# A third buffer for a unit's evacuated products, against shorter rings of sums, in a deformable-convolution block

## The chip, the cores and the metric

The kernel runs on one core of one Trainium2 chip. The metric is the device time of one execution in microseconds, the median of several runs. The profile is of one execution, whose span on the chip is 7707.8 us. PE is the matrix engine (TensorE), DVE is VectorE, ACT is ScalarE, POOL is GpSimd, and SP is the queue that issues nearly all DMAs.

## The reference

The input `x` is (2, 256, 128, 128) in fp32. The first layer normalises `x` by groups of channels, and runs three branches with dilations 1, 9 and 12. A branch computes 18 offsets per pixel by a 3x3 convolution, samples the image bilinearly at the nine displaced positions, and sums the nine samples with one weight per channel and tap. Then follow a norm over channels and a GELU. The three branches and a 1x1 convolution are added and go through a norm, a two-layer MLP and another norm. The second layer is a group norm and a 3x3 convolution with ternary weights. Cut to what matters here:

```
def _deform_dw(x, offset, w, pad, dil):
    ...
    py = yy[None, None] - pad + ky[None, :, None, None] * dil + off[:, :, 0]
    px = xx[None, None] - pad + kx[None, :, None, None] * dil + off[:, :, 1]
    sampled = _bilinear(x, py, px)
    wk = w.reshape(C, K)
    return jnp.einsum('bckhw,ck->bchw', sampled, wk)
def _branch(x, w_off, w_def, lw, lb, pad, dil):
    off = _conv(x, w_off, pad, dil)
    y = _deform_dw(x, off, w_def, pad, dil)
    return jax.nn.gelu(_ln2d(y, lw, lb), approximate=False)
...
out = _ln2d(x1 + x2 + x3 + c, n1_w, n1_b)
h = gelu(h @ mlp_w1.T + mlp_b1) @ mlp_w2.T + mlp_b2
```

## The kernel before

The kernel has three stages. The first writes a padded, transposed image to a table in DRAM, computes the offsets, and stores them as hat functions of the distance to each sampling position (`hats`), one set for y and one for x. The second samples and does the rest of the first layer. The third is the second layer's convolution. The change is in the second stage, `sample_near`, which takes the larger part of the time.

Sampling is done as a matrix product. A *unit* is an image, a pair of rows `Rt` and a branch `br`: 2 x 67 x 3 = 402 units. For a unit, DVE multiplies the hats in y with those in x into a matrix `A` (`build`, L813), once for each of the three kernel rows `ky`; the hats come by two loads, `hy` and `hx` (L793), with three buffers each, so that one unit fills them. The image's patches `xs` (L767) come as 14 loads for each pair of rows, into 20 buffers. A unit has two *samples*, one for each half of the channels (`sample(u, c)`). In a sample, PE multiplies the 14 patches by `A` (L886) in pairs, each pair into a PSUM bank `pm` (four banks); ACT copies each bank into `ev` (L895), the unit's evacuated products, in seven copies; and DVE adds them, tap by tap with a weight per channel, to sums held in a ring (`accumulate`, L864). The first product that reaches a row of the ring is written by ACT (L857) in place of an addition.

There is one ring for each branch, of `RINGS[br]` image rows (L50). A row `y` lies at `y % n_ring`. Two neighbouring rows are added by one instruction unless they cross the end of the ring, where the instruction is cut in two. When four rows (a *group*) have all their sums, the group's *tail* begins: PE transposes it out of the ring, ACT copies the transposes, and norms, GELU and, after the third branch, the MLP follow. The tails are advanced a step at a time between the samples by `tail.advance()`, so that their instructions are mixed with those of the sampling. If a new row would fall on ring rows whose group has not yet been transposed, the code advances the tail until it has:

```
while owner and owner != (b, br, m // R) and owner not in tail.read:
    tail.advance()
```

Nearly all instructions of PE, DVE and ACT in this stage are pinned to the order of the program (`pin`). On DVE the order within a unit is: the sums of the first half, then the builds of the unit after next (`prepare(u + 2)`), then the sums of the second half. `A` has two buffers, used in turn by the units. `ev` has two buffers:

```
ev = pool.tile([P, 9 * RI, NT * CI], F32, name="ev", tag="ev", bufs=2)
```

so ACT's first copy of a sample waits until DVE has done with the sums of the sample before the last. `load_hats(u + 1)` follows `prepare(u)`, and a scheduler sets the order of the loads on SP.

Of the kernel before, what the change touches and what calls it, by code (L numbers as in the profile page):

```python
# [9 lines left out]
F32 = mybir.dt.float32  # L10
# [9 lines left out]
P = 128  # L20
# [21 lines left out]
RI, CI = 2, 10  # L42
TR, TC = RI + 2 * REACH, CI + 2 * REACH
NT = -(-(W + 2 * REACH) // CI)
# [2 lines left out]
WA = 28 + W  # L47
NH = TR + TC
HALF = 64
RINGS = (12, 28, 32)  # L50
BRS = (0, 1, 2)
NORMS = 3
VBUFS = 9
# [14 lines left out]
def conv_preact_kernel(ctx: ExitStack, tc: tile.TileContext, t: dict, out: bass.AP):  # L68
# [680 lines left out]
    def sample_near(pool, psum, k):  # L749
# [26 lines left out]
        def taps(u):  # L776
            return [ky for ky in (-1, 0, 1) if valid(units[u][1], units[u][2], ky)]
# [43 lines left out]
        def accumulate(u, c, ev, kys):  # L821
# [4 lines left out]
            ring = k["rings"][br]  # L826
            n_ring = RINGS[br]
            sums = {ky: [] for ky in kys}
# [37 lines left out]
        def sample(u, c):  # L866

            b, Rt, br = units[u]
            kys = taps(u)
            tail.advance()  # L870
            if not kys:
                tail.advance()
                if c == KC - 1:
                    prepare(u + 2)
                return
            A = k["A"][u % len(k["A"])].rearrange("p t i w -> p (t i) w")
            m0, m1 = (kys[0] + 1) * 3 * RI, (kys[-1] + 2) * 3 * RI
            n = (m1 - m0) * CI
            ev = pool.tile([P, 9 * RI, NT * CI], F32, name="ev", tag="ev", bufs=2)
            for T in range(0, NT, 2):  # L880
                if T // 2 == NT // 4:
                    tail.advance()
                pm = psum.tile([P, 2, 256], F32, name="pm", tag="pm", bufs=4)
                for j in range(2):
                    pin(
                        nc.tensor.matmul(  # L886
                            pm[:, j, 0:n],
                            lhsT=xts[b, Rt][T + j][:, c * P : (c + 1) * P],
                            rhs=A[:, m0:m1, AO + (T + j) * CI : AO + (T + j + 1) * CI],
                            start=True,  # L890
                            stop=True,
                        )
                    )
                pin(
                    nc.scalar.copy(  # L895
                        ev[:, m0:m1, T * CI : (T + 2) * CI].rearrange(
                            "p m (t j) -> p t m j", j=CI
                        ),
                        pm[:, :, 0:n].rearrange("p t (m j) -> p t m j", j=CI),
                    )  # L900
                )
            if c == KC - 1:
                prepare(u + 2)
            accumulate(u, c, ev, kys)

        def prepare(u):

            if u < len(units):
                for ky in taps(u):
                    build(u, ky)  # L910
                if u + 1 < len(units):
                    load_hats(u + 1)
# [5 lines left out]
        for u, (b, Rt, br) in enumerate(units):  # L918
            if br == BRS[0] and u + len(BRS) < len(units):
                load_tiles(*units[u + len(BRS)][0:2])  # L920
            for c in range(KC):
                sample(u, c)

            while done[b, br] < NGRP and (
                Rt == NR - 1
                or (done[b, br] + 1) * R - 1 < (Rt + 1) * RI - REACH - DILS[br]
            ):
                g = done[b, br]
                r0 = g * R % RINGS[br]
                ring = k["rings"][br][:, :, r0 : r0 + R, :].rearrange("p k r w -> p k (r w)")  # L930
                tail.begin(tail.branch(b, br, g, ring), LAG)
                done[b, br] += 1
# [93 lines left out]
    with tc.If(beyond > 0) as cmp:  # L1026
        with ExitStack() as bctx:
            psum = bctx.enter_context(tc.tile_pool(name="ps_g", bufs=1, space=PSUM))
            pool = bctx.enter_context(tc.tile_pool(name="gpool", bufs=1))
            for b in range(NB):  # L1030
                sample_any(b, pool, psum)
    with cmp.Else():
        with ExitStack() as bctx:
            psum = bctx.enter_context(tc.tile_pool(name="ps_b", bufs=1, space=PSUM))
            pool = bctx.enter_context(tc.tile_pool(name="bpool", bufs=1))
# [3 lines left out]
            k["rings"] = [  # L1039
                pool.tile([P, KC, n, W], F32, name=f"ring{i}") for i, n in enumerate(RINGS)  # L1040
            ]
# [273 lines left out]
```

## Time and profile before

| | |
|---|---|
| median of 3 runs | 7720.23 us (7712.4 to 7721.3) |
| span of the profiled execution | 7707.8 us |
| PE busy | 7056.2 us, 92% |
| DVE busy | 6136.7 us, 80% |
| ACT busy | 4821.4 us, 63% |
| DMA, mean over the span | 215 GB/s |

Busy times are unions over the whole span, so they mix three stages with different limits. In the group lines of the page, the part after the first bar is the busy time in us and the mean duration of one instruction in ns (these overlap on PE), and the part after the second bar is the engine's idle time just before these instructions and what ended most of it. A line of the waits gives the waiting engine and its line, what it waited for, the total in us, how often, and the longest. A line of the timeline gives start and duration in us, and in square brackets the engine's idle time before it. A line of the windows gives for each stretch the busy time of PE, PE's weight load, DVE, ACT and POOL with their instructions, and then the granted clock of PE, the busy share of the DMA engines and GB/s.

### The profile page before, as it was taken

The numbers are of one execution on the slowest core, as the hardware profiler recorded it, in microseconds if no ns is written. First come the engines' busy times: TensorE is split into PE (matmuls) and PEld (weight loads), VectorE is DVE, ScalarE is ACT, GpSimd is POOL, SyncE is SP. The second block draws the span as 40 slices with busy tenths as digits, with TensorE's granted clock in tenths as the row PEclk, the third lists the DMA queues.
The fourth block names the chain that finished last, engine by engine and source line by source line (L and its number), as shares of the span: only waits on it lengthen the run. The fifth ranks groups of instructions, "written<-read, shape, count | busy, mean of one in ns | idle before, by whom it ended". The sixth has DMA issues, their size and how long they took to land. (4 is left out here: it accounts for less than half of the span.)

```text
span 7707.8 us, 115349 instructions
## 1 busy us (share of the span) xinstructions
PE 7056.2 (92%) x37984; PEld 5364.4 (70%) x37984; DVE 6136.7 (80%) x12907; ACT 4821.4 (63%) x10150; POOL 716.3 (9%) x1292
## 2 busy tenths in 40 slices
PE   6899888999999999999988999999999999899999
PEld 3455477877877787877777877877788877444444
DVE  7666658888888888888578888888888886677676
ACT  2344356777777777777666777777777777433232
POOL 0000000111111111111100111111111111000000
PEclk9899989999999999999999999999999999899999
DMA  9867699999999999998689999999999996222121
GB/s 296 242 188 200 181 233 252 243 254 257 248 250 254 255 246 249 248 255 228 190 232 249 250 250 258 248 251 252 251 249 251 246 250 172 86 77 73 71 74 49
DMA packets 1012350, 1658.94 MB, mean 215 GB/s; under 512 B 120672, under 2 KB 573072, under 8 KB 1007512
## 3 DMA queue, kind: packets, MB, share of 16 engines
q1 hardware_dynamic: 994328, 1617.86, 78.2%
q10 hardware_dynamic: 17408, 33.56, 1.3%
q8 instruction: 304, 4.98, 0.3%
q14 instruction: 310, 2.54, 0.1%
HBM read 1381.02 MB, written 270.06 MB: 214 GB/s over the span
## 5 line engine op out<-in xcount | busy, mean ns | idle before, releaser
L886 PE MATMUL pm<-A,xs 128*128 128x180 f32 (+2 forms) x22288 | 3603.7, 317 | 467.9 <-ACT ev L895 435.2
L886 PEld LDWEIGHTS pm<-A,xs 128*128 128x128 f32 x22288 | 3399.3, 195 | 684.4 <-ACT ev L895 543.7
L864 DVE SCALAR_TENSOR_TENSOR ring<-ev,defw,ring 128x256 f32<-128x256 f32 (+3 forms) x6272 | 2775.7, 462 | 358.6 <-ACT ev L895 173.4
L895 ACT COPY ev<-pm 128x360 f32<-128x360 f32 (+2 forms) x5572 | 2238.5, 455 | 1125.7 <-DVE ring L864 453.7
L813 DVE TENSOR_TENSOR A<-hy,hx 128x768 f32<-128x768 f32 x1130 | 1021.3, 946 | 417.4 <-DMA hx<-hats 238.6
L1169 PE MATMUL pc<-cring,signs 128*128 128x512 bf16 x4608 | 1007.5, 382 | 20.0 <-ACT cring L1116 13.3
L1169 PEld LDWEIGHTS <-signs 128*128 128x128 bf16 x4608 | 452.4, 98 | 574.5 <-issue 30.1
L611 ACT ACTIVATE T<-T,rs 128x256 f32<-128x256 f32 x1280 | 662.4, 593 | 3.3 <-POOL rs L607 3.2
L604 POOL TENSOR_SCALAR rs<-mv 128x4 f32<-128x4 f32 x320 | 122.5, 383 | 4962.3 <-DVE mv L602 2297.5
L570 PE MATMUL hp<-T,w 128*128 128x512 f32 x1024 | 493.1, 606 | 13.8 <-ACT T L689 13.8
L600 DVE BATCH_NORM_STATS2 st<-T 128x6 f32<-128x256 f32 x1280 | 447.0, 412 | 24.0 <-ACT T L592 23.9
L320 PE MATMUL pz<-wz,xa 128*128 128x486 f32 x1024 | 462.8, 585 | 1.3 <-DVE zr L327 1.3
L570 PE MATMUL h<-hT,w 128*128 128x512 f32 x1024 | 460.1, 592 | 0.0
L639 ACT ACTIVATE T<-zc,bb,bw 128x512 f32<-128x512 f32 x384 | 279.2, 782 | 219.8 <-PE zc L623 215.4
L857 ACT ACTIVATE ring<-ev,defw 128x256 f32<-128x256 f32 (+1 forms) x788 | 392.2, 503 | 24.1
L623 PEld LDWEIGHTS zc<-ident,T 128*128 128x128 f32 x2560 | 323.4, 150 | 97.2 <-issue 61.4
L1177 ACT ACTIVATE o<-xl,l1b 128x1024 f32<-128x1024 f32 x64 | 73.5, 1148 | 502.0 <-DMA out_x<-o 384.6
L623 PE MATMUL zc<-ident,T 128*128 128x128 f32 x2560 | 365.9, 287 | 20.2 <-ACT T L611 14.1
L606 POOL TENSOR_TENSOR rs<-rs,mhalf 128x4 f32<-128x4 f32 x320 | 371.3, 1160 | 0.0
L1116 ACT CAST cring<-D 128x2048 bf16<-128x2048 f32 (+1 forms) x140 | 245.0, 1755 | 185.0 <-PE pc L1169 127.6
L592 ACT COPY T<-tp 128x512 f32<-128x512 f32 x640 | 341.9, 590 | 29.5 <-PE tp L590 29.2
L427 ACT ACTIVATE hb<-ph 96x512 f32<-96x512 f32 (+1 forms) x384 | 211.2, 592 | 183.0 <-PE ph L419 177.0
(118 smaller groups left out, 5258.8 us busy)
## 6 DMA issues: line engine op xcount, KB each, us to landing
hy<-hats SPq DMA_DIRECT2D x1114, 384.0 KB
hx<-hats SPq DMA_DIRECT2D x1114, 384.0 KB
xs<-table SPq DMA_DIRECT2D x1876, 128.0 KB
g12d<-T SPq DMA_DIRECT2D x128, 512.0 KB
other<-g12d SPq DMA_DIRECT2D x128, 512.0 KB
hats<-hb SPq DMA_DIRECT2D x192, 240.0 KB
hats<-hb SPq DMA_DIRECT2D x192, 192.0 KB
xl<-x1d SPq DMA_DIRECT2D x56, 640.0 KB
```

The costliest lines, as they stand in the source:

```text
L320: nc.tensor.matmul(pz[:, 0:NZ], lhsT=xt[:, c, r, :], rhs=k["wz"][:, c, :], start=c == 0, stop=c == KC - 1,)
L570: nc.tensor.matmul(out, lhsT=w, rhs=v, start=i == 0, stop=i == n - 1)
L600: pin(nc.vector.bn_stats(st[:, j, :], Tv[:, j, :]))
L606: nc.gpsimd.tensor_tensor(rs[:, 0, :], rs[:, 0, :], mhalf[:, 0:NB4], ALU.pow)
L611: nc.scalar.activation(Tv[:, j, :], Tv[:, j, :], AF.Identity, scale=rs[:, 0, j : j + 1], bias=rs[:, 1, j : j + 1],)
L623: nc.tensor.transpose(zc[:, j * P : (j + 1) * P], Tv[:, j, c * P : (c + 1) * P], ident)
L813: nc.vector.tensor_tensor(dst, hy[:, i0:i1].rearrange("p i t w -> p t i w"), hx[:, i0:i1].rearrange("p i t w -> p t i w"), ALU.mult,)
L857: pin(nc.scalar.mul(dst, src, w))
L864: pin(nc.vector.scalar_tensor_tensor(dst, src, w, dst, ALU.mult, ALU.add))
L886: nc.tensor.matmul(pm[:, j, 0:n], lhsT=xts[b, Rt][T + j][:, c * P : (c + 1) * P], rhs=A[:, m0:m1, AO + (T + j) * CI : AO + (T + j + 1) * C ...
L895: nc.scalar.copy(ev[:, m0:m1, T * CI : (T + 2) * CI].rearrange("p m (t j) -> p t m j", j=CI), pm[:, :, 0:n].rearrange("p t (m j) -> p t m ...
L1169: nc.tensor.matmul(pc[:, bank, :], lhsT=w[:, m * P : (m + 1) * P], rhs=xc[:, i, k, t * JC : (t + 1) * JC, kx : kx + W], start=j == 0, stop ...
```

## The change

`ev` gets a third buffer, and two rings lose four rows each. Each `ev` buffer takes 18 x 140 x 4 = 10080 bytes of a partition, and a ring row 2 x 128 x 4 = 1024 bytes, so eight rows are 8192 bytes.

```diff
-RINGS = (12, 28, 32)
+RINGS = (8, 24, 32)
...
-            ev = pool.tile([P, 9 * RI, NT * CI], F32, name="ev", tag="ev", bufs=2)
+            ev = pool.tile([P, 9 * RI, NT * CI], F32, name="ev", tag="ev", bufs=3)
```

ACT's first copy of a sample then waits for the sums of the sample three before it. In the rings of dilation 1 and dilation 9 a group's rows are taken again one group earlier, and row pairs cross the end of these rings more often.

## The prediction

> **What bounds the kernel now.** I read the page's slices first, to find the stage that the change touches.
>
> ```profile
> PE   6899888999999999999988999999999999899999
> DVE  7666658888888888888578888888888886677676
> DMA  9867699999999999998689999999999996222121
> GB/s 296 242 188 200 181 233 252 243 254 257 248 250 254 255 246 249 248 255 228 190 232 249 250 250 258 248 251 252 251 249 251 246 250 172 86 77 73 71 74 49
> ```
>
> A slice is 193 us. Slices 6 to 33 are the sampling stage, with PE at 9, DVE at 8 and DMA at 9 at once; no engine stands alone. The dip in the middle is where image 0 ends and image 1 begins. Then the groups:
>
> ```profile
> L886 PE MATMUL pm<-A,xs 128*128 128x180 f32 (+2 forms) x22288 | 3603.7, 317 | 467.9 <-ACT ev L895 435.2
> L864 DVE SCALAR_TENSOR_TENSOR ring<-ev,defw,ring 128x256 f32<-128x256 f32 (+3 forms) x6272 | 2775.7, 462 | 358.6 <-ACT ev L895 173.4
> L895 ACT COPY ev<-pm 128x360 f32<-128x360 f32 (+2 forms) x5572 | 2238.5, 455 | 1125.7 <-DVE ring L864 453.7
> ```
>
> The chain of releases is the point: PE waits for ACT to empty a PSUM bank (435.2 us), and ACT waits for DVE to finish with an `ev` (453.7 us). The waits in the even part of the stage, 2000 to 3500 us:
>
> ```profile
> ACT ev L895 <- PE pm L886: 113.3, 51, 3.0
> PE pm L886 <- ACT ev L895: 100.7, 67, 3.1
> ACT ev L895 <- DVE ring L864: 99.1, 65, 2.9
> DVE ring L864 <- ACT ev L895: 42.4, 25, 2.1
> DVE A L813 <- DMA hx<-hats: 36.6, 33, 2.9
> DVE A L813 <- PE pm L886: 35.8, 14, 2.6
> ```
>
> PE idles 104 us of these 1500 (busy 1395.9), and 100.7 of it is this one wait. DVE waits for PE and ACT (42.4 + 35.8 + 18.5 for h = 96.7 us), and for hats (36.6). So each waits for the other, at different places. The timeline shows where. The work repeats: the same 2.56 us wait stands at 3045.33 and 3131.77, so a period (two row steps, six units) is 86.4 us.
>
> ```profile
> 3131.77 2.70 DVE L813 TENSOR_TENSOR A<-hy,hx 128x768 f32<-128x768 f32 x3 [2.56 <-PE pm L886]
> 2107.41 3.77 DVE L864 SCALAR_TENSOR_TENSOR ring<-ev,defw,ring 128x256 f32<-128x256 f32 x8 [2.08 <-ACT ev L895]
> 2134.21 1.19 ACT L895 COPY ev<-pm 128x360 f32<-128x360 f32 x3 [2.16 <-DVE ring L864]
> 2134.72 2.10 PE L886 MATMUL pm<-A,xs 128*128 128x180 f32 x12 [2.38 <-ACT ev L895]
> 2146.11 3.12 ACT L895 COPY ev<-pm 128x360 f32<-128x360 f32 x7 [2.01 <-DVE ring L864]
> 2146.63 2.10 PE L886 MATMUL pm<-A,xs 128*128 128x180 f32 x12 [1.12 <-ACT ev L895]
> 2154.12 1.19 ACT L895 COPY ev<-pm 128x360 f32<-128x360 f32 x3 [1.43 <-DVE ring L864]
> 2154.64 2.10 PE L886 MATMUL pm<-A,xs 128*128 128x180 f32 x12 [2.59 <-ACT ev L895]
> ```
>
> From 2107 to 2154 DVE runs without a wait for PE or ACT and holds both back; in the other 39 us of the period PE works on the tail's long matmuls, and DVE waits. Two buffers let ACT be one sample ahead, which is too little to carry PE over the DVE-heavy part. One whole period by windows:
>
> ```profile
> 2107.00:2193.40 86.40, 79.63 (x461) 67.83 (x460) 75.59 (x171) 65.13 (x145) 11.37 (x20) 1.00 0.96 251
> ```
>
> **What the Trainium skill says.** "Perfetto Trace Analysis", Optimization Strategy: the same gap coming back on the engine that should be saturated can mean too few buffers. That is this picture: three PE gaps in each period, each just after ACT's wait for an `ev`. The same page, Identifying the Most-Contended Engine, calls DMA occupancy misleading, since there are 16 engines. The trace agrees: in stretches of 5 us the share goes up to 1.12, so I use bytes. "VectorE: DVE Perf Modes", The TRN2 errata, says that an operation on SBUF pays a fixed cost per instruction. Here 128x256 takes 481 ns and 128x128 takes 346 ns, so halving a row pair costs 2 x 346 - 481 = 211 ns.
>
> **The change part by part.**
>
> *Third `ev`.* ACT's first copy of sample s then waits for the sums of sample s-3, not s-2. One sum of 8 instructions (3.8 us) and what DVE does beside it lie between the two. The waits to be removed are 2.2 us at most, so all of them go at the present timing. What PE gets back is the smaller of each pair above: 2.16 + 1.12 + 1.43 = 4.7 us per period. The rest of PE's gaps (0.2, 1.2 and 0.4 us at 2106.35) is ACT busy with copies of the tail, and stays. PE's floor is 86.4 - 4.7 = 81.7 us.
>
> *The other floors.* DVE's waits for PE and ACT in this period are 4.1 + 2.6 + 0.7 = 7.4 us (waits by engine), so DVE could do it in 79.0, plus 0.3 for the splits below. DMA moves 251 GB/s x 86.4 us = 21.7 MB; over the 188 of 290 five-us windows with a share of 1.00 or more the rate was 267 GB/s on average, so it needs 81.2 us even if never idle. Three floors within 2.5 us mean that none will be met. Hats are the weak point: `hy` and `hx` have three buffers each, which one unit fills, so the next unit's loads cannot start before this unit's builds. I take two thirds of the 4.7: 3.1 us per period, a period of 83.3 us at 260 GB/s. The share is a choice: at nothing, DMA bounds; at all of it, PE does.
>
> *How many periods.* Even stretches are 1450 to 3450 and 4200 to 6200 us: 4000 / 86.4 = 46.3. So 46.3 x 3.1 = 144 us. At the starts of the images (1200 to 1450, 3950 to 4200) DVE is held by hats (27.0 and 37.9 us of 250) and by neither PE nor ACT (under 4 us); the waits for `ev` there are slack, so I count nothing. Ends of images: nothing, up to 10 us.
>
> *Shorter rings: splits.* A row pair that crosses a ring's end is cut in two. Counted from the built program: 64 of 128x256 become 128 of 128x128, and 8 of 2x122 become 16 of 122: 64 x 0.211 + 8 x (2 x 0.338 - 0.473) = 15.1 us of DVE. In the even stretches DVE has 7.4 us of slack per period against 0.3. On the path: some 2 us, at the starts. Bounds: 0 and 15.
>
> *Shorter rings: waits.* The rows of a ring are taken again a group earlier, and the code then advances the tail until the old rows have been transposed. In the built programs PE, ACT and POOL have the same instructions in the same order before and after, so no advance is forced. ACT writes the first product of a new row only after its own copy of those transposes, so no wait is added: 0, at most 15 us if some region is tracked more coarsely.
>
> *SP's order.* At the images' starts, 16 blocks of eight `xs` loads in all move ahead of one to four hats loads. In the even part, in each period, one `hy` load moves behind a block of eight `xs`; its `hx` stood behind that block before. An `xs` load waits for PE to free a buffer, and hats stand behind it on SP; DVE's build waits for those, its sums behind the build, and then ACT and PE. Eight issues took 5.18 us (from 3005.30), so the starts can lose 0 to 16 x 5.2 = 83 us. In the even part the build waits for the later of the two loads, and now both come after the block: 384 KB at 267 GB/s is 1.5 us, so 0 to 46 x 1.5 = 69 us. I take 0 for both: DVE's floor of 79.3 us lies 2.4 us under PE's, which hides 1.5; and at the starts a faster PE frees the `xs` buffers sooner.
>
> Sum, against the profiled span: 7707.8 - 144 + 2 = 7566 us. The three runs shown have their median 12.4 us above that span, so 7578.
>
> **The rivals.**
>
> *PE takes all (15%).* 46.3 x 4.7 = 218 us, with up to 20 from the ends: 7480 to 7540. For it: DVE's slack is larger than PE's gain. Against it: 251 x 86.4 / 81.7 = 265 GB/s, almost the rate of the full windows.
>
> *DMA bounds (20%).* At the images' starts, where hats visibly hold DVE, DMA makes 251 GB/s, no more than in the even part. If this is what the loop of build, free, load and build allows, DVE's waits for PE turn into waits for hats: 0 to 2.2 us per period, 7605 to 7720. Against it: in the even part hats hold DVE only 2.4 us of 86.
>
> *Slower (10%, a quarter of it within the bound).* SP's new order: `xs` ahead of hats, up to 83 us at the starts and 69 us in the even part, as just worked out. At the starts hats are nearly DVE's only wait, so a later load goes through to the end. It decides if it costs more than the third buffer gives: with half of it exposed (76 us), if the even part gains under 60 us. Then 7735 to 7800. Against it: SP waits for DVE's builds for 474.8 us of the 1500 (SP's own waits), so a block ahead of hats often goes out in time that was idle.
>
> *The likeliest (55%).* 2.4 to 3.9 us per period: 7540 to 7609.
>
> **How the numbers follow.** About 0.2%, 15 us, can be told from no change. Faster by more: 0.55 + 0.15 + 0.16 of the DMA case = 0.86. Within it: 0.04 of the DMA case and 0.03 of the slower one, 0.07. Slower: 0.07. The range, 7500 to 7690, leaves out about 0.06 below and 0.13 above.
>
> **What would show it.** In the changed profile: ACT's wait for ring L864 falls from 453.7 us to under 150, and what is left lies at the images' starts; PE's wait for ev falls from 100.7 to under 50 in 1500 us; the period shrinks to 83.3; DMA goes to about 260 GB/s; DVE's waits for PE and ACT fall from 96.7, its waits for hats rise. L864 has 72 more instructions. I am wrong if ACT's wait is gone and the period stays (then look at hats), or if PE's gap stays behind ACT's tail copies.

## The result, and the profile after

The changed kernel takes 7633.0 us (median of four runs, 7630.3 to 7650.2) against 7720.8: a ratio of 0.9893, with a 95% interval of 0.9876 to 0.9911. That is a gain of 88 us; the profiled spans, 7629.6 against 7707.8 us, differ by 78. The forecast was 7578. So the sign and the range were right, and the gain came out at about three fifths of what was worked out.

The groups of the page after, the same lines as before and two more (L813, L611):

```profile
L886 PE MATMUL pm<-A,xs 128*128 128x180 f32 (+2 forms) x22288 | 3613.3, 318 | 350.8 <-ACT ev L895 250.1
...
L864 DVE SCALAR_TENSOR_TENSOR ring<-ev,defw,ring 128x256 f32<-128x256 f32 (+3 forms) x6344 | 2779.0, 459 | 335.9 <-ACT ev L895 155.7
L895 ACT COPY ev<-pm 128x360 f32<-128x360 f32 (+2 forms) x5572 | 2243.6, 449 | 777.9 <-PE pm L886 451.9
L813 DVE TENSOR_TENSOR A<-hy,hx 128x768 f32<-128x768 f32 x1130 | 1025.6, 946 | 403.2 <-DMA hx<-hats 278.1
...
L611 ACT ACTIVATE T<-T,rs 128x256 f32<-128x256 f32 x1280 | 661.9, 589 | 183.5 <-POOL rs L607 183.4
```

The releaser of L895 has changed: it was DVE's ring with 453.7 us, and is now PE. PE's wait for ACT fell from 435.2 to 250.1 us, but it has not gone. L864 has the 72 more instructions of the splits. The last line is new: ACT waits 183.4 us for a scale `rs` that POOL computes for a norm in the tail. Before, this wait was 3.2 us in all. DVE's wait for hats rose from 238.6 to 278.1 us.

The waits in the even part, 2000 to 3500 us, of the kernel after:

```profile
PE pm L886 <- ACT ev L895: 57.8, 48, 3.9
ACT T L611 <- POOL rs L607: 50.0, 18, 3.9
DVE A L813 <- DMA hx<-hats: 49.1, 41, 3.0
...
DVE ring L864 <- ACT ev L895: 36.7, 19, 2.1
...
DVE A L813 <- PE pm L886: 31.7, 19, 2.6
...
PE pm L886 <- DMA xs<-table: 10.4, 15, 1.8
```

ACT's wait for DVE's ring (99.1 us before) is no longer in the list. In its place stand 50.0 us of ACT for POOL, 12.5 us more of DVE for hats, and 9.3 us more of PE for the patches. The same stretch by windows:

```profile
2000.00:3500.00 1500.00, 1427.27 (x8130) 1208.98 (x8129) 1335.06 (x3012) 1148.87 (x2530) 202.10 (x356) 0.99 0.96 254
```

PE's idle time fell from 104 to 73 us of 1500. DMA rose from 250 to 254 GB/s, where 260 had been forecast.

To measure the period on many repeats, I took the mean time of 18 builds (L813; six units of three builds are a period) over each of the two even stretches. It fell from 86.03 and 86.08 us to 84.61 and 84.32: from 86.05 to 84.47 on average, so 1.6 us. Times 46.3 periods this is 73 us. The start of image 0 (its first 174 builds) gave 4.7 us more, and the change from image 0 to image 1 (builds 516 to 678) 3.0, so 81 us against the 78 of the spans: the gain is where it was expected, in the even part.

The timeline after shows both new waits within one stretch:

```profile
3073.67 1.39 DVE L600 BATCH_NORM_STATS2 st<-T 128x6 f32<-128x256 f32 x4
...
3074.97 0.36 DVE L602 BATCH_NORM_AGGREGATE mv<-st 128x2 f32<-128x6 f32 x4
...
3075.50 0.30 POOL L604 TENSOR_SCALAR rs<-mv 128x4 f32<-128x4 f32 x1 [7.78 <-DVE mv L602]
...
3077.37 0.29 POOL L607 TENSOR_TENSOR rs<-rs 128x4 f32<-128x4 f32 x1
...
3077.70 2.08 ACT L611 ACTIVATE T<-T,rs 128x256 f32<-128x256 f32 x4 [2.38 <-POOL rs L607]
...
3080.18 2.10 PE L886 MATMUL pm<-A,xs 128*128 128x180 f32 x12 [1.76 <-ACT ev L895]
...
3081.89 0.96 DVE L813 TENSOR_TENSOR A<-hy,hx 128x768 f32<-128x768 f32 x1 [1.17 <-DMA hx<-hats]
...
3084.43 0.51 SPq L793 DMA_DIRECT2D hy<-hats  x1
...
3084.99 0.59 SPq L793 DMA_DIRECT2D hx<-hats  x1
...
3095.24 0.96 DVE L813 TENSOR_TENSOR A<-hy,hx 128x768 f32<-128x768 f32 x1 [1.29 <-DMA hx<-hats]
```

First the norm: DVE's statistics start at 3073.67, POOL has the scale ready only at 3077.66, and ACT stands 2.38 us in front of L611. The copies of products (L895) are queued behind it, so PE waits 1.76 us at 3080.18. ACT used to reach L611 later, because it had waited for DVE on the way; now it comes there ahead of the scale. Then the hats: the third build of a unit ends at 3082.85, its buffers are loaded again by the issues at 3084.43 and 3084.99, the build that waited for them starts 10.2 us after the second issue, and it ends at 3096.20. One round of this loop took 13.35 us, and a unit has 84.47 / 6 = 14.1 us on average. The loop has almost no slack left.

Most rounds in which DVE waits for hats are longer than this one, because the loads are issued late:

```profile
2184.22 10.37 SPq L767 DMA_DIRECT2D xs<-table  x13
2189.50 2.69 DVE L813 TENSOR_TENSOR A<-hy,hx 128x768 f32<-128x768 f32 x3
...
2198.37 0.52 SPq L793 DMA_DIRECT2D hy<-hats  x1
2198.94 0.58 SPq L793 DMA_DIRECT2D hx<-hats  x1
...
2207.61 0.96 DVE L813 TENSOR_TENSOR A<-hy,hx 128x768 f32<-128x768 f32 x1 [1.74 <-DMA hx<-hats]
```

The third build ends at 2192.19, but SP is still issuing patches and other hats, and the second load of its buffers goes out only 6.8 us later. The round is 16.4 us. Over the 37 waits for hats of more than 0.3 us from 2000 to 3450 us, the median time from a free buffer to the issue of `hx` is 6.6 us; in the builds without such a wait it is 1.0.

### The profile page after: what moved, and what is told of

It is laid out like the page before. It is cut to its first block, busy times and chain, and to the rows that moved or that the text cites. A ratio compares the mean times of both kernels' runs of the same rounds, so it can differ in the third digit from the quotient of the medians.

```text
span 7629.6 us, 115662 instructions
## 1 busy us (share of the span) xinstructions
PE 7073.0 (93%) x37984; PEld 5344.6 (70%) x37984; DVE 6140.8 (80%) x12979; ACT 4827.6 (63%) x10150; POOL 710.2 (9%) x1292
## 5 line engine op out<-in xcount | busy, mean ns | idle before, releaser
L886 PE MATMUL pm<-A,xs 128*128 128x180 f32 (+2 forms) x22288 | 3613.3, 318 | 350.8 <-ACT ev L895 250.1
L864 DVE SCALAR_TENSOR_TENSOR ring<-ev,defw,ring 128x256 f32<-128x256 f32 (+3 forms) x6344 | 2779.0, 459 | 335.9 <-ACT ev L895 155.7
L895 ACT COPY ev<-pm 128x360 f32<-128x360 f32 (+2 forms) x5572 | 2243.6, 449 | 777.9 <-PE pm L886 451.9
L813 DVE TENSOR_TENSOR A<-hy,hx 128x768 f32<-128x768 f32 x1130 | 1025.6, 946 | 403.2 <-DMA hx<-hats 278.1
L611 ACT ACTIVATE T<-T,rs 128x256 f32<-128x256 f32 x1280 | 661.9, 589 | 183.5 <-POOL rs L607 183.4
L600 DVE BATCH_NORM_STATS2 st<-T 128x6 f32<-128x256 f32 x1280 | 446.8, 411 | 21.8 <-ACT T L592 21.7
L623 PE MATMUL zc<-ident,T 128*128 128x128 f32 x2560 | 353.3, 281 | 20.3 <-ACT T L611 14.1
```

Source lines behind the costliest of these rows:

```text
L600: pin(nc.vector.bn_stats(st[:, j, :], Tv[:, j, :]))
L611: nc.scalar.activation(Tv[:, j, :], Tv[:, j, :], AF.Identity, scale=rs[:, 0, j : j + 1], bias=rs[:, 1, j : j + 1],)
L623: nc.tensor.transpose(zc[:, j * P : (j + 1) * P], Tv[:, j, c * P : (c + 1) * P], ident)
L813: nc.vector.tensor_tensor(dst, hy[:, i0:i1].rearrange("p i t w -> p t i w"), hx[:, i0:i1].rearrange("p i t w -> p t i w"), ALU.mult,)
L864: pin(nc.vector.scalar_tensor_tensor(dst, src, w, dst, ALU.mult, ALU.add))
L886: nc.tensor.matmul(pm[:, j, 0:n], lhsT=xts[b, Rt][T + j][:, c * P : (c + 1) * P], rhs=A[:, m0:m1, AO + (T + j) * CI : AO + (T + j + 1) * C ...
```

## The experiments

My theory was that the third `ev` does what was said, and that something which the removed wait had covered takes part of the gain back. There were three candidates for the taker: the tail's norm (DVE, POOL, ACT), DMA's bandwidth, and the depth of the loop of hats. A fourth was that the shorter rings or their splits cost more than the 2 us allowed.

**The rings alone.** The kernel after with two `ev` again:

```diff
-            ev = pool.tile([P, 9 * RI, NT * CI], F32, name="ev", tag="ev", bufs=3)
+            ev = pool.tile([P, 9 * RI, NT * CI], F32, name="ev", tag="ev", bufs=2)
```

> The kernel before with rings of 8, 24 and 32 rows and ev left at two buffers: the ring part alone. Theory: 15 us of DVE work, mostly hidden, so 0 to +15 us against before. Rival (shorter rings cost more than the splits, by SP's order or a wait on old rows, and ate part of the gain): +30 us or more.

Measured: 7712.9 us, a ratio of 0.9989 (0.9979 to 0.9999) to the kernel before, and a period of 86.06 us. The splits and the earlier reuse of rows cost nothing that can be measured, and the fourth candidate falls. This run has nearly the order of loads on SP of the kernel before, so it doesn't test the new order, which came with the third `ev`.

**A longer pause ahead of the norm's scaling.** The tail pauses between a norm's statistics (L600) and its scaling (L611). I made this pause two steps longer, in the kernel after and, as a control, in the kernel before:

```diff
-            yield 5
+            yield 7
```

> The changed kernel, with the tail's pause between a norm's statistics and its scaling raised from 5 steps to 7, so that ACT reaches the scaling a sample later. Theory (norm chain: the new wait ACT T L611 <- POOL rs, 183 us in all, took back what the third ev gave): that wait falls under 40 us, and PE gets back up to the 1.8 us per period that stood behind it, 46 x 1.8 = 80 us: 7540 to 7600. Rival (the loop of hats loads and builds sets the period): the wait falls too, the time stays at 7615 to 7650, and DVE's wait for hats grows in its place.

> The kernel before with the pause of 7 steps. There ACT waits for POOL 3 us in all, so the norm-chain theory expects nothing: within 0.3% of before (7700 to 7745). If the longer pause helps by itself, by a better mixing of the tail, it gains here too: under 7690.

Measured: 8018.0 us (ratio 1.039, 1.0367 to 1.0413) and 8055.0 us (1.0448, 1.0419 to 1.0477). The wait for `rs` did fall, to 6.7 us in all. But the control, which hardly had that wait, lost 334 us where the first lost 385, so the pair says nothing about the norm. The pause shifts the order on all engines: in the first of the two ACT waits 87.3 us of 1450 for loads of `xn`, and PE 60.0 us for DVE's L738, which neither kernel did to that extent. To test a wait by moving the waiting step was the wrong tool; the next pair leaves the order alone.

**The norm without its chain.** Statistics and scaling stay as instructions, with the same sizes and in the same places, but wait for nothing, so the norms are left out. (DVE's statistics then don't wait for ACT's copies of the transposes either, which took 21.7 us in all in the kernel after.)

```diff
-                pin(nc.vector.bn_stats(st[:, j, :], Tv[:, j, :]))
+                pin(nc.vector.bn_stats(st[:, j, :], convs[0][:, 0, :]))
...
-                        scale=rs[:, 0, j : j + 1], bias=rs[:, 1, j : j + 1],
+                        scale=mhalf[:, 0:1], bias=mhalf[:, 1:2],
```

> The changed kernel with the tail's norms cut loose from their statistics: DVE takes the statistics of a constant tile and ACT scales by constants (the norms are left out), with the same instructions in the same order on PE, ACT and DVE, so that ACT never waits for POOL. Norm-chain theory: ACT T L611 <- POOL rs goes from 183 us to 0, and PE gets back most of the 1.8 us per period behind it: 7545 to 7590. Hats-loop rival: the wait goes, but the time stays at 7615 to 7640, and DVE's wait for hats rises above its 49 us in 1500.

> The same cut in the kernel before, as a control. ACT waited for POOL 3 us in all there: no change is expected by either theory, 7695 to 7740.

Measured, on the kernel after: 7617.1 us, a ratio of 0.9859 (0.9837 to 0.9882), so only 16 us less than the kernel after, and a period of 84.31 us. On the kernel before: 7713.3 us, 0.9985 (0.9976 to 0.9994). This control hardly has the wait and gained 7.5 us too, and 0.16 us of its period, as much as the first; so at most a part of the 16 us is the norm's wait. The waits of the kernel after, and below them those of the first run, from 2000 to 3450 us (the faster kernels reach the end of image 0 earlier, so their stretch is 50 us shorter):

```profile
PE pm L886 <- ACT ev L895: 53.4, 45, 3.9
...
DVE A L813 <- DMA hx<-hats: 46.1, 40, 2.1
...
PE pm L886 <- DMA xs<-table: 9.7, 14, 1.8
```

```profile
DVE A L813 <- DMA hx<-hats: 90.0, 71, 2.5
...
PE pm L886 <- DMA xs<-table: 39.9, 21, 4.8
...
PE pm L886 <- ACT ev L895: 23.0, 31, 2.4
```

ACT's wait at L611 is gone, and PE's wait for `ev` fell from 53.4 to 23.0 us. But hats, which held DVE for 46.1 us, now hold it for 90.0, and patches, which held PE for 9.7 us, hold it for 39.9. The time went from one wait into two others. As the only taker the norm falls; whether it is a second one behind the loads was left for a later run.

**Fewer bytes.** Every second pair of rows uses the patches of the pair before, which takes away about 8% of the bytes, and half of the `xs` issues on SP:

```diff
         def load_tiles(b, Rt):
+            if Rt % 2:
+                xts[b, Rt] = xts[b, Rt - 1]
+                return
```

> The changed kernel without the loads of patches for every second row pair (it uses the patches of the pair before): 8% fewer bytes in the sampling stage, all else the same. Norm-chain theory: ACT's wait for POOL stays, only PE's small wait for xs (10 us in 1500) goes: 7590 to 7635. Hats-loop rival: DVE's wait for hats falls by half or more and the time to 7550 or less.

> The kernel before without every second load of patches. If the bytes bound only the changed kernel, it gains little here, under 50 us (7670 to 7720); if DMA held both alike, it gains as much as the changed kernel did (7632 to 7538, 95 us): 7610 to 7640.

Measured, on the kernel after: 7538.2 us, 0.9763 (0.9741 to 0.9784), period 83.36; on the kernel before: 7650.2 us, 0.9905 (0.9878 to 0.9933), period 85.56. So even the kernel before gains 70 us, which lies between the two outcomes that had been named (56 us by the profiled spans, of which 21 us at the first image's start and 14 at the second's). The third `ev` is worth 7650.2 - 7538.2 = 112 us here, against 88. Loads are a taker. But this edit relieves the bytes, SP and the hats' landing at once, so it can't say what about the loads it is.

**Both edits together**, on the kernel after and on the kernel before:

> The changed kernel with the norms cut loose and every second load of patches left out. If the norm chain and DMA each hold a part of their own, the gains add: 7460 to 7500. If one bound stands behind the other, the time stays within 20 us of the better of the two alone.

> The kernel before with the norms cut loose and every second load of patches left out, the partner of the run with both in the changed kernel (7467). If the third ev is worth what the step of the prediction said (4.7 us per period at most, 218 us) once DMA and the norm chain are out of the way, this is at 7620 to 7650, 155 to 185 us above. If the freed parts help the two-buffer kernel alike: under 7570.

Measured: 7466.6 us, 0.9653 (0.9628 to 0.9678), period 82.19; and 7653.7 us, 0.9921 (0.9902 to 0.9941), period 85.57. The waits of the first, from 2000 to 3450 us (the edit moves the line numbers by three):

```profile
DVE A L816 <- DMA hx<-hats: 57.9, 52, 2.2
...
PE pm L889 <- DMA xs<-table: 22.8, 13, 2.7
...
PE pm L889 <- ACT ev L898: 13.5, 23, 2.4
```

The norm's chain, worth 16 us when taken away alone, is worth 7538.2 - 7466.6 = 72 us once loads are fewer. So it is a taker, and stands behind the loads. With both out of the way the third `ev` gives 187 us, or 3.4 us per period, and PE's wait for `ev` is nearly gone. In the kernel with two `ev`, removing the norm's chain on top of the patches changed nothing (7650.2 and 7653.7).

**The depth of the loop of hats, at the same bytes.** `hy` and `hx` get four buffers each, so that the load for the next unit's first build need not wait for this unit's builds. With two `ev` and the shorter rings there is room for it; with three `ev` the room comes from stand-in weights:

```diff
-                hy = pool.tile([P, RI, 3, W], F32, name="hy", tag="hy", bufs=3)
-                hx = pool.tile([P, RI, 3, W], F32, name="hx", tag="hx", bufs=3)
+                hy = pool.tile([P, RI, 3, W], F32, name="hy", tag="hy", bufs=4)
+                hx = pool.tile([P, RI, 3, W], F32, name="hx", tag="hx", bufs=4)
...
-    w2 = load("w2", [P, MC, C], t["w2"].rearrange("(k p) o -> p k o", p=P))
+    w2 = w1.rearrange("p k (q o) -> p (k q) o", o=C)
```

The last two lines, and one copy of the 1x1 weights for both images, belong to the kernel with three `ev` only.

> The short rings, ev at two buffers, and the memory spent on a fourth buffer for hy and hx instead. If the depth of the hats loop is what holds DMA and DVE, hats wait less (44 us in 1500 before) but PE's wait for ev stays, since ev is as before: 7660 to 7700, less than the third ev gives. If hats hold the kernel before more than ev does: under 7633.

> The changed kernel with a fourth buffer for hy and hx; the room comes from the constants: the second MLP matrix is read from the first one's memory, and both images share one set of 1x1 weights (so these products are not the reference's). Same instructions otherwise. If the hats loop's depth (loads that cannot start before the builds) is the bound that is left: DVE's wait for hats falls under 25 us in 1500 and the time to 7540 to 7590, like with fewer bytes. If it is bandwidth alone: the wait stays near 45 us and the time within 20 us of 7633.

Measured: with two `ev` 7656.3 us, 0.9915 (0.9899 to 0.9931), period 85.78; with three 7522.5 us, 0.9743 (0.9723 to 0.9763), period 83.14. Both lie a little under the ranges expected. (Hats held the kernel before for 36.6 us of 1500, not for 44.) The waits of the second from 2000 to 3450 us, where lines are one lower:

```profile
PE pm L885 <- ACT ev L894: 53.9, 52, 3.1
...
DVE A L812 <- PE pm L885: 42.3, 19, 2.6
DVE ring L863 <- ACT ev L894: 34.3, 17, 2.1
ACT T L610 <- POOL rs L606: 31.9, 18, 3.0
```

No wait for hats of any size is left (0.9 us), and nothing else had to be taken away. The same stretch by windows, the kernel after and then this run:

```profile
2000.00:3450.00 1450.00, 1382.17 (x7828) 1168.27 (x7826) 1291.14 (x2907) 1110.28 (x2436) 194.85 (x344) 0.99 0.96 255
```

```profile
2000.00:3450.00 1450.00, 1384.54 (x8006) 1179.05 (x8005) 1314.84 (x2975) 1133.64 (x2494) 202.19 (x352) 1.00 0.97 259
```

DMA ran at 259 GB/s with a share of 0.97, where the kernel after has 255 and 0.96. The sampling moves the same bytes, 110 us sooner. So bandwidth was not the limit at 255 GB/s; the three buffers of a loop with no slack, and the order of issue that went with them, were. With four buffers the scheduler also orders the loads on SP anew; how much of the gain is depth and how much is order, the run doesn't tell. With two `ev`, deeper hats bring 64 us, mostly at the images' starts, and leave ACT's wait for DVE (79.4 us) and PE's for `ev` (96.6 us of 1450) in place.

**A version that might be faster still.** Four buffers for hats and three `ev`, with room made from one copy of the 1x1 weights, whose scale ACT applies instead, and from 16 buffers for `xs` in place of 20:

```diff
-                xt = pool.tile([P, C], F32, name="xs", tag="xs", bufs=20)
+                xt = pool.tile([P, C], F32, name="xs", tag="xs", bufs=16)
```

> A version that computes the reference: the changed kernel with four buffers for hy and hx. The room comes from the 1x1 weights, kept once (the image's scale goes into the ACT operation that centres x), and from xs at 16 buffers in place of 20. If the depth of the hats loop is what is left and PE does not miss the four xs buffers: 7515 to 7560. If xs at 16 holds PE (its wait for xs over 40 us in 1500, hats queued behind xs on SP): 7580 to 7640, no better than the changed kernel.

Measured: 7638.5 us, 0.9879 (0.9858 to 0.9901), no better than the kernel after; the period is 84.57. PE now waits 41.9 us of 1450 for patches (9.7 in the kernel after), hats still hold DVE for 23.5, and the change from image 0 to image 1 takes 896 us instead of 880. By these waits, what four hats buffers gave, four fewer patch buffers took. The run with 16 patch buffers alone was not made, and ACT's scaling changed with them, so this is read from the waits and not shown.

The medians come from several sessions, in which that of the kernel before lay between 7713 and 7726 us, so differences of a few us between rows mean nothing. What the third `ev` brings, by what else is relieved (medians in us, period in us; the kernels with two `ev` have the long rings, but for the last row, which the rings-only run makes comparable):

| relieved | two `ev` | three `ev` | gain | period |
|---|---|---|---|---|
| nothing | 7720.8 | 7633.0 | 88 | 86.05 to 84.47 |
| norm | 7713.3 | 7617.1 | 96 | 85.89 to 84.31 |
| patches | 7650.2 | 7538.2 | 112 | 85.56 to 83.36 |
| patches and norm | 7653.7 | 7466.6 | 187 | 85.57 to 82.19 |
| depth of hats | 7656.3 | 7522.5 | 134 | 85.78 to 83.14 |

## Why the prediction was right, and where its size was off

*The mechanism* was right. ACT's wait for DVE's ring fell from 453.7 to 70.4 us, where under 150 had been forecast; none of it is in the even stretches: 41.4 us stand before 1450 us, at the start of image 0, and 29.0 from 3450 to 4200, where image 0 ends and image 1 begins. PE's wait for `ev` fell, from 5.8 us per period (100.7 x 86.05 / 1500) to 3.3, where under 50 us in 1500 had been forecast and 57.8 came. "Perfetto Trace Analysis", Optimization Strategy, in the Trainium skill says that a gap that keeps coming back can mean too few buffers; the trace bears it out (with a third buffer ACT's 99.1 us are gone), but the gap was worth less than its length.

*The mis-sized term* is "two thirds of the 4.7: 3.1 us per period". It measured 1.6. The time lies outside the range called likeliest (7540 to 7609, at 55%) and inside that of a rival at 20%; only the wide range, 7500 to 7690, held it. PE's wait for `ev` gave 2.5 us back; 0.5 went to waits for patches, and some 0.3 into busy time of PE (1395.91 x 86.05 / 1500 = 80.1 against 1427.27 x 84.47 / 1500 = 80.4). Two loops took what is missing, 1.5 us. The one that comes first is the loop of hats. The prediction named it as the weak point, with its three buffers, but priced it through bandwidth (81.2 us at 267 GB/s) and not through the round itself, which took 13.35 us and often more, of 14.1. With a fourth buffer the period is 83.14 us at 259 GB/s: the forecast had 83.3 at 260. That these agree is in part luck, since the share of two thirds was a choice, and the norm's wait is still there (31.9 us of 1450). The second is one that the prediction did not name: ACT, no longer held by DVE, arrives at the norm's scaling before DVE and POOL have made the scale, so a wait for DVE's sums became a wait for DVE's statistics. Removed alone it gave 16 us, half of which its control gained too; removed after the patches it gave 72, where the control (7650.2 and 7653.7 us) gained nothing. With patches and norm both relieved, the third `ev` gives 3.4 us per period, and the period is 82.19 us, near the floor of 81.7 that was worked out for PE. But its partner with two `ev` has 85.57 and not 86.4, so 3.4 of the 4.7 came back and not all.

*The floors of DVE and DMA.* DVE's waits for PE and ACT fell from 96.7 to 69.7 us (36.7 + 31.7 + 1.3 for `h`), and its wait for hats rose, as forecast. "Three floors within 2.5 us mean that none will be met" held in the kernel after, though not for the reason given: two loops held the period, and not the closeness of the floors.

*The rings.* 2 us on the path, with bounds of 0 and 15: nothing measurable. The 15.1 us of DVE behind them were too many: L864's busy time rose by 3.3 us (2775.7 to 2779.0), and by 5.8 with the rings alone. The 15.1 came from mean durations, which overlap: the 488 instructions of 128x128 in the kernel after have a mean of 346 ns but keep DVE busy for 140.3 us, 288 ns each. "VectorE: DVE Perf Modes", The TRN2 errata, in the Trainium skill speaks of a fixed cost per instruction; the 72 extra instructions pay it, 3.3 us in all, and here it lies in DVE's slack. The ends of the images: near nothing, as taken; the starts gave 5 and 3 us where none was counted.

*SP's order*, taken at 0. Blocks of `xs` issues are part of the round of hats in both kernels. Of the 18 waits for hats over 0.3 us between 2000 and 2700 us in the kernel after, 8 have seven or eight `xs` issues between the free buffer and the issue of its load, 6 have two to four, and 4 have none; of the 13 in the kernel before, it is 8, 1 and 4. Behind the blocks of seven or eight, the place that the prediction named, DVE loses 9.5 us after and 10.0 before, so no new loss shows there. What is new are the six at the end of a block of thirteen, 9.2 us against 0.4. That block stands in both kernels. But in the kernel before one or two of it are still to be issued when DVE's build frees the buffer, and in these six waits mostly four, so the load behind them goes out later after the build, and DVE waits for it. The slower rival's loss does not show: the starts gained, and so did the even part. No run has the new order alone, so its effect by itself was not measured.

*The rival "DMA bounds"* holds the measured time in its range (7605 to 7720), and half of its mechanism: waits for hats do take the place of waits for PE. Its text named the loop of build, free, load and build, which was right; its title named bytes, which was not. Too few buffers for the loop held it, and the rival left out the norm. "PE takes all" fell: it needed both loops out of the way.

What stays open: how much of the norm's 72 us would be had with four hats buffers and all patches, which wasn't tried. The tests of the norm and of the patches also overlap at SP, so the shares of the two takers are no exact split of the 1.5 us. Nor was it tried whether three buffers would do if SP issued the hats ahead of the patches.

## What to carry to other kernels

When a buffer removes a wait, follow the engine that is now early: list what it reaches next in its order, and ask when each of these inputs is ready, down to the small engines (here 2.2 us of POOL for a scale). Price a prefetch loop by its round (free, issue, land, use) against the time of a unit, not only by bytes per second. Waits in series hide each other, so an experiment that removes one of them may show little (16 us, and 7.5 in its control); remove it again with the next one gone (72 us) before calling it free.

## What was unexpected in the hardware

The DMA share hardly tells a bound loop from a free one: 0.96 at 255 GB/s in the kernel after, and 0.97 at 259 in the kernel with deeper hats, which is 110 us faster. "Perfetto Trace Analysis", Identifying the Most-Contended Engine, in the Trainium skill calls this occupancy misleading, and these two runs agree. And in this traffic (255 GB/s) a build that waited for a load of 384 KB began 6.1 to 12.2 us after the load's issue, with a median of 8.9 over 37 such waits: most of the 14.1 us of a unit.
